# Both modulations at once, and the constants ahead of them, at the head of a two-layer adaLN kernel

## The chip, the cores and the metric

The kernel is one program for one core of a Trainium2 chip. The metric is the device time of one execution in microseconds (us). Three runs of the kernel before took 4933.53, 4936.85 and 4939.53 us; the median is 4936.85.

The engines are named as in the profile: PE is TensorE (PEld its weight loads), DVE is VectorE, ACT is ScalarE, POOL is GpSimd, and SP is the engine that issues all DMAs of this kernel.

## The reference

The state x has 4096 rows of 128 features, as two sequences of 2048 rows for the outer layers. Two layers, L0 and L1, each modulate a mixer ("attn") and a feed-forward model ("ffn") by a vector c:

```
mod = (silu(c) @ wmod).reshape(2, 6, 1, 128)         # c: 2 x 128, wmod: 128 x 768
sa, ca, ga, sb, cb, gb = mod[:, 0] ... mod[:, 5]
ga = (2*(ga >= 0) - 1) * max(|ga|, 0.25)              # gb the same
h = layernorm(x) * (1 + ca) + sa;   x = x + ga * attn(h)
h = layernorm(x) * (1 + cb) + sb;   x = x + gb * ffn(h)
```

The attention of L0 has 16 heads of 8 features and works on chunks of 64 rows: softmax attention inside a chunk, plus 0.1 times q times a memory matrix M per head. M is carried through the chunks by a delta rule, row by row: M = M - alpha * (M k) k^T + beta * v k^T, with k normalised to length 1, alpha = sigmoid(alpha_raw) * 0.5 and beta = sigmoid(beta_raw) * 2. The ffn of L0 is a model of six local attention layers with feed-forward parts; L1 has a linear attention and a model of two such layers.

## The kernel before

The program first makes a few constants (`ident`, `ones`, `onesm`, `nhalf`, `identb`, `cen`), then computes the modulation vectors of both layers, then the attention of L0 (`l0_attention`), then everything else in `local_models`. The change is in the first 90 us of the program.

**Modulation** (L130 to L159). `modulation(pre)` is called for L0 and then for L1, each with a memory pool of its own that is freed at its end. It loads `wmod` (128 x 768, 384 KB) and c (128 x 2), forms c * sigmoid(c) with an Exp on ACT (L136) and three small DVE operations (L137 to L140), does six matmuls (L143) into one PSUM bank, copies the 12 columns out (L147), adds 1 to two of the six vectors (L149), and applies the sign and floor rule to two others (L153 to L158, six DVE operations of 128 x 2 each). Since the second pool takes the memory of the first, the second load of `wmod` waits for the first modulation, and the attention's constants, whose pool takes the same memory, wait for the second.

**Constants of the attention** (L190 to L213). Six loads on SP: `wT` (the three projections' weights, 192 KB), `WoT`, `headsel`, `mask_chunk`, `na` (alpha, one value per partition), and `be` (beta, 128 values given to all 128 partitions). From `na` and `be` the two sigmoids are made (Exp on ACT at L200, then L201 to L203 on DVE), and from `wT` and `be` the weights `wkv` of the key and value projection (L212, L213).

**Projection stage** (L215 to L331). From `manual_schedule()` on (L216), each engine's order is the order in which the code is written; ahead of it, a scheduler orders the instructions. The 4096 rows are four groups of 1024 for the input norm and eight blocks of 512 for the rest:

- four loads of `xt` (128 x 8 x 128, 512 KB each, L318) on SP;
- `norm(g)`: the mean on DVE (`mu`, L238), the subtraction on POOL (`xn`, L241), a Square on ACT (`sq`, L243), the variance on DVE (`ve`, L245), the power -0.5 on POOL (`rt`, L248) and the product on POOL (`xn`, L249);
- `dims_first(blk)`: four transposes on PE of `xt` and four of `xn` (L257), ACT copies the first to `xb`, which SP stores to DRAM (`xD`, L127), and writes the modulated second to `hT` (L265);
- `project(blk)`: matmuls of `hT` with `wkv` (L274) and of `wT` with `hT` for q (L280), three ACT operations (`ksq` L284, `vt` L285, `qT` L286), a reduction and a polynomial for 1 / |k| on DVE (L289, L167 to L180) and the normalised key `kn` (L296);
- `keys(blk)`: four transposes of `kn` (L307), the ACT copy to `kT` (L308), and two DMAs on SP that regroup the keys through DRAM (`kdr` L309, `kr` L311).

The order of these steps is a written loop:

```
            norm(0)
            for j in range(-1, 9):
                if j in (-1, 1, 3):
                    norm((j + 3) // 2)
                if j + 1 < 8:
                    dims_first(j + 1)
                if 0 <= j < 8:
                    project(j)
                if 1 <= j:
                    keys(j - 1)
```

so that a norm's ACT operation stands in ACT's queue ahead of the copies of the block that follows it. `xt` and `xn` have four and two buffers; PSUM banks for the transposes, q and the keys are three, taken in turn.

**Behind the head.** The recursion over the rows of a chunk (`step`, L361 to L376, on DVE) begins when `kr` has been regrouped into `kd` (L347), beside the softmax attention of 32 tiles of 128 rows; then follow the chain over the chunks, the output projection, and the local models. Their order is written out by hand, too.

Of the kernel before, what the change touches and what calls it, by code (L numbers as in the profile page):

```python
# [72 lines left out]
def tile_kernel(ctx: ExitStack, tc: tile.TileContext, a: dict, out: bass.AP):  # L73
# [12 lines left out]
    @contextmanager  # L86
    def banks(name):

        with tc.tile_pool(name=name, bufs=2, space=PSUM) as p:
            cur[0] = p  # L90
            yield p
# [35 lines left out]
        nc.sync.dma_start(xD[:, blk * 512:(blk + 1) * 512], t)  # L127


    def modulation(pre):  # L130
        m = keep.tile([128, 6, 2], F32, name=f"{pre}_m")
        with tc.tile_pool(name=f"{pre}_modp", bufs=1) as mp, banks(f"{pre}_psm"):
            w = load(f"{pre}_wmod", (128, 768), mp)
            c = load(f"{pre}_cT", (128, 2), mp)
            e = mp.tile([128, 2], F32, name="e")
            nc.scalar.activation(e, c, AF.Exp, scale=-1.0)  # L136
            nc.vector.tensor_scalar(e, e, 1.0, None, ALU.add)  # L137
            s = mp.tile([128, 2], F32, name="s")
            nc.vector.reciprocal(s, e)
            nc.vector.tensor_tensor(s, s, c, ALU.mult)  # L140
            pm = ps("A")
            for k in range(6):
                nc.tensor.matmul(  # L143
                    pm[:, 2 * k:2 * k + 2], lhsT=w[:, k * 128:(k + 1) * 128], rhs=s,
                    start=True, stop=True,
                )
            nc.vector.tensor_copy(m.rearrange("p k b -> p (k b)"), pm[:, 0:12])  # L147
            for k in (1, 4):
                nc.vector.tensor_scalar(m[:, k, :], m[:, k, :], 1.0, None, ALU.add)  # L149
            for k in (2, 5):  # L150
                g = mp.tile([128, 2], F32, name="g")
                n = mp.tile([128, 2], F32, name="n")
                nc.vector.tensor_scalar(g, m[:, k, :], 0.0, 2.0, ALU.is_ge, ALU.mult)  # L153
                nc.vector.tensor_scalar(g, g, -1.0, None, ALU.add)
                nc.vector.tensor_scalar(n, m[:, k, :], -1.0, None, ALU.mult)
                nc.vector.tensor_tensor(n, n, m[:, k, :], ALU.max)
                nc.vector.tensor_scalar(n, n, 0.25, None, ALU.max)
                nc.vector.tensor_tensor(m[:, k, :], g, n, ALU.mult)  # L158
        return m  # L159


    def rsqrt_quick(scr, n, pool):
# [22 lines left out]

    def l0_attention(m):

        cp = ctx2.enter_context(tc.tile_pool(name="a_c", bufs=1))  # L190
        wT = load("L0_attn_wT", (128, 3, 128), cp)
# [20 lines left out]
        nc.vector.tensor_copy(wkv[:, 0], wT[:, 1, :])  # L212
        nc.vector.tensor_tensor(wkv[:, 1], wT[:, 2, :], be, ALU.mult)  # L213

        hp = ctx2.enter_context(tc.tile_pool(name="a_h", bufs=1))  # L215
        ctx2.enter_context(tc.manual_schedule())  # L216
        hT = hp.tile([128, T], F32, name="hT")
# [11 lines left out]
        with tc.tile_pool(name="a_p", bufs=2) as wp, tc.tile_pool(  # L229
            name="a_psP", bufs=2, space=PSUM  # L230
        ) as pp:
            P = {}

            def norm(g):

                xt = P["xt", g]
                mu = wp.tile([128, 8], F32, name="mu")
                nc.vector.tensor_reduce(mu, xt, AX.X, ALU.add)  # L238
                nc.vector.tensor_scalar(mu, mu, 1.0 / 128.0, None, ALU.mult)
                xn = P["xn", g] = wp.tile([128, 8, D], F32, name="xn")  # L240
                nc.gpsimd.tensor_tensor(xn, xt, bc(mu.unsqueeze(2), (128, 8, D)), ALU.subtract)  # L241
                sq = wp.tile([128, 8, D], F32, name="sq", bufs=1)
                nc.scalar.activation(sq, xn, AF.Square)  # L243
                ve = wp.tile([128, 8], F32, name="ve")
                nc.vector.tensor_reduce(ve, sq, AX.X, ALU.add)  # L245
                nc.vector.tensor_scalar(ve, ve, 1.0 / 128.0, 1e-5, ALU.mult, ALU.add)
                rt = wp.tile([128, 8], F32, name="rt")
                nc.gpsimd.tensor_tensor(rt, ve, bc(nhalf, (128, 8)), ALU.pow)  # L248
                nc.gpsimd.tensor_tensor(xn, xn, bc(rt.unsqueeze(2), (128, 8, D)), ALU.mult)  # L249

            def dims_first(blk):
                b = blk // NBLK
                ts_ = []
                for nm in ("xt", "xn"):
                    pt = pp.tile([128, 512], F32, tag="T", name="ps_x", bufs=3)
                    for c in range(4):
                        nc.tensor.transpose(  # L257
                            pt[:, c * 128:(c + 1) * 128],
                            P[nm, blk // 2][:, 4 * (blk % 2) + c, :], ident,
                        )  # L260
                    ts_.append(pt)
                xb = wp.tile([128, 512], F32, name="xb")
                nc.scalar.copy(xb, ts_[0])
                store_x(blk, xb)
                nc.scalar.activation(  # L265
                    hT[:, blk * 512:(blk + 1) * 512], ts_[1], AF.Identity,
                    bias=m[:, 0, b:b + 1], scale=m[:, 1, b:b + 1],
                )

            def project(blk):  # L270
                n0 = blk * 512
                pk = pp.tile([128, 4, 2, 128], F32, tag="K", name="ps_k")
                for c in range(4):
                    nc.tensor.matmul(  # L274
                        pk[:, c].rearrange("p s f -> p (s f)"),
                        lhsT=hT[:, n0 + c * 128:n0 + (c + 1) * 128],
                        rhs=wkv.rearrange("p s f -> p (s f)"), start=True, stop=True,
                    )
                pq = pp.tile([128, 512], F32, tag="T", name="ps_q", bufs=3)
                nc.tensor.matmul(  # L280
                    pq, lhsT=wT[:, 0, :], rhs=hT[:, n0:n0 + 512], start=True, stop=True
                )
                ksq = wp.tile([128, 4, 128], F32, name="ksq")
                nc.scalar.activation(ksq, pk[:, :, 0, :], AF.Square)  # L284
                nc.scalar.copy(vt[:, 4 * blk:4 * blk + 4, :], pk[:, :, 1, :])  # L285
                nc.scalar.mul(qT[:, n0:n0 + 512], pq, 1.0 / math.sqrt(8.0))  # L286

                ss = pp.tile([128, 4, 64], F32, tag="R", name="ps_r", bufs=1)
                nc.vector.tensor_reduce(  # L289
                    ss[:, 0], ksq.rearrange("p c (h d) -> p (c h) d", d=8), AX.X, ALU.add  # L290
                )
                rk = rsqrt_quick([ss[:, k] for k in range(4)], 64, wp)
                kn = P["kn", blk] = wp.tile([128, 4, 128], F32, name="kn")
                for c in range(4):
                    v = lambda t: t.rearrange("p (h d) -> p h d", d=8)
                    nc.vector.scalar_tensor_tensor(  # L296
                        v(kn[:, c]), v(pk[:, c, 0]), RSQ_C,
                        bc(rk[:, 16 * c:16 * c + 16].unsqueeze(2), (128, 16, 8)),
                        ALU.mult, ALU.mult,
                    )  # L300

            def keys(blk):
                sl = slice(blk * 512, (blk + 1) * 512)
                pt = pp.tile([128, 512], F32, tag="T", name="ps_kt", bufs=3)
                kn = P.pop(("kn", blk))
                for c in range(4):
                    nc.tensor.transpose(pt[:, c * 128:(c + 1) * 128], kn[:, c], ident)  # L307
                nc.scalar.copy(kT[:, sl], pt)  # L308
                nc.sync.dma_start(kdr[:, sl], kT[:, sl])  # L309
                v = kdr[0:16, sl]  # L310
                nc.sync.dma_start(  # L311
                    kr[blk:blk + 121:8, :, :],
                    bass.AP(v.tensor, v.offset, [[8 * T, 16], [T, 8], [1, 512]]),
                )

            for g in range(4):
                xt = P["xt", g] = wp.tile([128, 8, D], F32, name="xt", bufs=4)
                nc.sync.dma_start(  # L318
                    xt, a["x"][g * 1024:(g + 1) * 1024, :].rearrange("(c p) d -> p c d", p=128)
                )  # L320
            norm(0)
            for j in range(-1, 9):
                if j in (-1, 1, 3):
                    norm((j + 3) // 2)
                if j + 1 < 8:
                    dims_first(j + 1)
                if 0 <= j < 8:
# [3 lines that stand above are left out]
# [369 lines left out]
        assert done == len(todo)  # L700
        for f in finish(3):
            f()
        return E["hs"]

# [831 lines left out]
        while lsteps:  # L1538
            lstep()

    m0 = modulation("L0")
    m1 = modulation("L1")
    with ExitStack() as ctx2:
        hs0 = l0_attention(m0)
    with ExitStack() as ctx2:
        local_models(m0, m1, hs0)

# [62 lines left out]
```

## Time and profile before

| | us |
|---|---|
| median of three runs | 4936.85 |
| lowest and highest | 4933.53, 4939.53 |
| the profiled execution | 4928.13 |
| its span in the profile | 4926.3 |
| PE busy | 4493.8 (91%) |
| DVE busy | 3949.1 (80%) |
| POOL busy | 2781.2 (56%) |
| ACT busy | 2637.9 (54%) |
| first projection matmul starts | 34.99 |
| last `kT` copy starts | 87.06 |

The profile is of one execution. Times in its timeline count from the start of the span. Engines run their instructions in order; where an engine was idle before an instruction, the timeline gives the idle time and what released it, in brackets. The rows of windows give the length, then busy time with the number of instructions for PE, PEld, DVE, ACT and POOL, then the clock granted to PE, the share of the DMA engines that was busy, and GB/s. In this profile a matmul of two f32 operands is two records, a transpose one.

### The profile page before, as it was taken

What the parts mean: (1) busy time and instruction counts of PE and PEld (TensorE: products, weight loads), DVE (VectorE), ACT (ScalarE), POOL (GpSimd) and SP (SyncE); (2) the same over time, 40 slices, a digit from 0 to 9 for tenths busy, and PEclk for the clock granted to TensorE, in tenths of its full rate; (3) what the DMA queues carried; (4) which work ended last, traced back from release to release, by engine and by line L of the source; (5) the groups of instructions that cost most, each with busy time, mean ns of one, the idle gap of its engine ahead of it and who ended that gap; (6) DMA issues with size and microseconds to landing.
All of it is one profiled execution on the core that took longest, in us unless ns stands there. A gap on an engine that the chain in (4) does not pass through costs nothing.

```text
span 4926.3 us, 166334 instructions
## 1 busy us (share of the span) xinstructions
PE 4493.8 (91%) x73028; PEld 3066.5 (62%) x73058; DVE 3949.1 (80%) x6840; ACT 2637.9 (54%) x4207; POOL 2781.2 (56%) x1666
## 2 busy tenths in 40 slices
PE   5667799999999999999999999999999998899997
PEld 4445566666666666666666666666666665556554
DVE  6994488888888888888887888888877777788886
ACT  3223355555555555555555555555555555465554
POOL 3332366666666666666666666666655544455552
PEclk8778899999999999999999999999999999999999
DMA  2000222222222322223222322222212111111121
GB/s 78 1 1 25 85 65 67 69 73 70 69 65 64 87 68 65 66 73 76 68 64 64 79 72 65 66 74 69 68 51 59 50 51 46 37 46 49 51 58 41
DMA packets 222468, 295.31 MB, mean 60 GB/s; under 512 B 75657, under 2 KB 95409, under 8 KB 221745
## 3 DMA queue, kind: packets, MB, share of 16 engines
q1 hardware_dynamic: 221744, 284.67, 22.4%
q8 instruction: 576, 9.44, 0.8%
q14 instruction: 148, 1.20, 0.1%
HBM read 40.98 MB, written 10.75 MB: 10 GB/s over the span
## 4 chain that ended last, share of the span: by engine, by line
PE 49%; DVE 25%; ACT 7%; POOL 5%; issue 3%; DMA 0%; SPq 0%; POOLq 0%; DVEq 0%; ACTq 0%
PE ps_qk L871 12%; PE ps_o L1050 5%; PE ps_v L957 5%; DVE ps_qk L899 5%; PE ps_f L1150 5%; DVE t L888 5%; PE ps_turn L938 4%; PE ps_y L1067 4%; POOL r L894 4%; PE ps_s L997 3%; DVE r L883 3%; PE ps_fy L1175 3%; ACT sq L873 2%; DVE rs L1021 2%; PE ps_pT L1032 2%
## 5 line engine op out<-in xcount | busy, mean ns | idle before, releaser
L894 POOL TENSOR_TENSOR r<-r,t 128x1024 f32<-128x1024 f32 x448 | 1060.2, 2367 | 911.8 <-DVE t L888 794.3
L906 POOL TENSOR_TENSOR r<-r,rq_y 128x1024 f32<-128x1024 f32 x448 | 843.8, 1902 | 517.9 <-DVE rq_y L180 495.8
L873 ACT ACTIVATE sq<-ps_qk 128x1024 f32<-128x1024 f32 x448 | 460.6, 1028 | 1082.3 <-PE ps_qk L871 1014.7
L871 PE MATMUL ps_qk<-wp,hs 128*128 128x512 f32 x1792 | 893.8, 621 | 105.7 <-DVE rq_y L180 77.1
L883 DVE TENSOR_TENSOR r<-ps_qk,tb 128x1024 f32<-128x1024 f32 (+1 forms) x512 | 550.7, 1076 | 211.8 <-ACT sq L873 198.4
L1050 PEld LDWEIGHTS ps_o<-pT,v 64*64 64x64 f32 (+1 forms) x26624 | 479.4, 136 | 304.5 <-ACT pT L1033 160.9
L888 DVE TENSOR_TENSOR t<-ps_qk,tb 128x1024 f32<-128x1024 f32 (+1 forms) x512 | 554.1, 1082 | 143.1 <-POOL r L894 142.4
L1023 POOL TENSOR_TENSOR sm<-sm,rs 128x1024 f32<-128x1024 f32 x256 | 487.5, 1904 | 210.2 <-DVE rs L1022 126.9
L1050 PE MATMUL ps_o<-pT,v 64*64 64x32 f32 (+1 forms) x26624 | 531.2, 221 | 37.0 <-ACT pT L1033 19.2
L899 DVE TENSOR_REDUCE ps_qk<-sq 128x16 f32<-128x1024 f32 x448 | 549.0, 1226 | 11.9
L871 PEld LDWEIGHTS ps_qk<-wp,hs 128*128 128x128 f32 x1792 | 310.1, 193 | 364.3 <-issue 236.1
L938 PEld LDWEIGHTS ps_turn<-ident,r 128*128 128x128 f32 x3584 | 411.7, 143 | 125.2 <-issue 99.4
L957 PE MATMUL ps_v<-wp,hs 128*128 128x512 f32 x896 | 481.9, 639 | 1.0 <-ACT oT L1056 0.8
L1067 PEld LDWEIGHTS ps_y<-oT,wo 128*128 128x128 f32 x3584 | 430.2, 193 | 46.9 <-issue 42.5
L938 PE MATMUL ps_turn<-ident,r 128*128 128x128 f32 x3584 | 447.3, 277 | 9.7 <-POOL r L906 4.1
L1067 PE MATMUL ps_y<-oT,wo 128*128 128x128 f32 x3584 | 446.3, 276 | 1.5 <-ACT oT L1056 1.5
L1056 ACT COPY oT<-ps_o 128x512 f32<-128x512 f32 x448 | 244.0, 588 | 281.9 <-PE ps_o L1050 281.2
L1005 DVE TENSOR_REDUCE mx<-ps_s 128x16 f32<-128x1024 f32 (+1 forms) x256 | 312.5, 1221 | 97.4 <-PE ps_s L997 95.6
L997 PE MATMUL ps_s<-kT,qT 64*32 64x64 f32 (+1 forms) x26624 | 377.9, 230 | 0.7 <-issue 0.5
L997 PEld LDWEIGHTS ps_s<-kT,qT 64*32 64x32 f32 (+1 forms) x26624 | 325.8, 107 | 63.7 <-issue 53.0
L1150 PE MATMUL ps_f<-fx,w 128*128 128x512 f32 (+1 forms) x768 | 356.1, 600 | 2.5 <-DVE fx L1133 1.7
L1021 DVE TENSOR_REDUCE rs<-sm 128x16 f32<-128x1024 f32 (+1 forms) x256 | 310.5, 1213 | 51.1 <-ACT sm L1014 49.0
(265 smaller groups left out, 6850.5 us busy)
## 6 DMA issues: line engine op xcount, KB each, us to landing
v<-vn SPq DMA_DIRECT2D x1276, 128.0 KB
v<-vn SPq DMA_DIRECT2D x744, 64.0 KB
v<-vn SPq DMA_DIRECT2D x64, 256.0 KB
wp<-in_L_ffn_Wqkv SPq DMA_DIRECT2D x20, 512.0 KB
xD<-xb SPq DMA_DIRECT2D x24, 256.0 KB
xb<-xD SPq DMA_DIRECT2D x24, 256.0 KB
cs<-in_cos SPq DMA_DIRECT2D x128, 32.0 KB
cs<-in_sin SPq DMA_DIRECT2D x128, 32.0 KB
```

The source lines that it names most:

```text
L871: nc.tensor.matmul(pq[:, js], lhsT=hw, rhs=wts[g, u][:, js], start=True, stop=True)
L883: nc.vector.tensor_tensor(r[:, es].rearrange("p (h d) -> p h d", d=DH), pq[:, es].rearrange("p (h d) -> p h d", d=DH), bc(tb[:, 0, s].unsq ...
L888: nc.vector.tensor_tensor(t2[:, es].rearrange("p (h s d) -> p h s d", s=2, d=32), pq[:, es].rearrange("p (h s d) -> p h s d", s=2, d=32)[: ...
L894: nc.gpsimd.tensor_tensor(r, r, t2, ALU.add)
L899: nc.vector.tensor_reduce(pq[:, 16 * v:16 * v + 16], st[i].pop(("sq", v)).rearrange("p (h d) -> p h d", d=DH), AX.X, ALU.add,)
L906: nc.gpsimd.tensor_tensor(rv, rv, bc(y[:, 16 * v:16 * v + 16].unsqueeze(2), (128, 16, DH)), ALU.mult)
L938: nc.tensor.transpose(p[:, c * 128:(c + 1) * 128], r[:, cs], ident)
L957: nc.tensor.matmul(p, lhsT=hw, rhs=wv, start=True, stop=True)
L997: nc.tensor.matmul(sp[W * w:W * w + W, c0:c0 + 2 * W], lhsT=qT[64 * q:64 * q + 64, cc, W * w:W * w + W], rhs=kT[64 * q:64 * q + 64, cc, W ...
L1050: nc.tensor.matmul(po[s][64 * q:64 * q + 64, 128 * c + W * w:128 * c + W * w + W], lhsT=v2[kp, w, co:co + 64], rhs=pT[kp, q, c, W * w:W * ...
L1067: nc.tensor.matmul(py[:, 0:128], lhsT=wts[g, "o"][:, c * NO + s, :], rhs=oT[:, s, c, :], start=(c + s == 0), stop=(c == 3 and s == NO - 1),)
L1150: nc.tensor.matmul(ps_[c][0:sz], lhsT=wts[g, "w1"][:, o:o + sz], rhs=S["x"], start=True, stop=True,)
```

## The change

One function now makes both modulations. It loads c and `wmod` of both layers, does each small operation once on 128 x 4 values instead of twice on 128 x 2, does the twelve matmuls one after another, and leaves both results in one tile. It is called inside `l0_attention`, behind the loads and the preparation of the attention's constants and ahead of the projection stage. The second and third input norm are given out one turn of the loop sooner, and `xn` has four buffers instead of two.

```diff
-    def modulation(pre):
-        m = keep.tile([128, 6, 2], F32, name=f"{pre}_m")
-        with tc.tile_pool(name=f"{pre}_modp", bufs=1) as mp, banks(f"{pre}_psm"):
-            w = load(f"{pre}_wmod", (128, 768), mp)
-            c = load(f"{pre}_cT", (128, 2), mp)
-            e = mp.tile([128, 2], F32, name="e")
+    def modulation():
+        m = keep.tile([128, 2, 6, 2], F32, name="m")
+        with tc.tile_pool(name="modp", bufs=1) as mp, banks("psm"):
+            c = mp.tile([128, 2, 2], F32, name="c")
+            ws = []
+            for i, pre in enumerate(("L0", "L1")):
+                nc.sync.dma_start(c[:, i, :], a[f"{pre}_cT"])
+                ws.append(load(f"{pre}_wmod", (128, 768), mp))
+            e = mp.tile([128, 2, 2], F32, name="e")
             nc.scalar.activation(e, c, AF.Exp, scale=-1.0)
...
             pm = ps("A")
-            for k in range(6):
-                nc.tensor.matmul(
-                    pm[:, 2 * k:2 * k + 2], lhsT=w[:, k * 128:(k + 1) * 128], rhs=s,
-                    start=True, stop=True,
-                )
-            nc.vector.tensor_copy(m.rearrange("p k b -> p (k b)"), pm[:, 0:12])
+            for i in range(2):
+                for k in range(6):
+                    o = 12 * i + 2 * k
+                    nc.tensor.matmul(
+                        pm[:, o:o + 2], lhsT=ws[i][:, k * 128:(k + 1) * 128], rhs=s[:, i, :],
+                        start=True, stop=True,
+                    )
+            nc.vector.tensor_copy(m.rearrange("p i k b -> p (i k b)"), pm[:, 0:24])
             for k in (1, 4):
-                nc.vector.tensor_scalar(m[:, k, :], m[:, k, :], 1.0, None, ALU.add)
+                nc.vector.tensor_scalar(m[:, :, k, :], m[:, :, k, :], 1.0, None, ALU.add)
             for k in (2, 5):
...
-        return m
+        return m[:, 0], m[:, 1]
...
-    def l0_attention(m):
+    def l0_attention():
...
         nc.vector.tensor_tensor(wkv[:, 1], wT[:, 2, :], be, ALU.mult)
 
+        m, m1 = modulation()
         hp = ctx2.enter_context(tc.tile_pool(name="a_h", bufs=1))
...
-                xn = P["xn", g] = wp.tile([128, 8, D], F32, name="xn")
+                xn = P["xn", g] = wp.tile([128, 8, D], F32, name="xn", bufs=4)
...
-                if j in (-1, 1, 3):
-                    norm((j + 3) // 2)
+                if j in (-1, 0, 2):
+                    norm({-1: 1, 0: 2, 2: 3}[j])
...
-        return E["hs"]
+        return E["hs"], m, m1
...
-    m0 = modulation("L0")
-    m1 = modulation("L1")
     with ExitStack() as ctx2:
-        hs0 = l0_attention(m0)
+        hs0, m0, m1 = l0_attention()
```

More of the change, by code (lines that the diff above doesn't have):

```diff
@@ L127, in store_x @@
         nc.sync.dma_start(xD[:, blk * 512:(blk + 1) * 512], t)
-    def modulation(pre):
-        m = keep.tile([128, 6, 2], F32, name=f"{pre}_m")
-        with tc.tile_pool(name=f"{pre}_modp", bufs=1) as mp, banks(f"{pre}_psm"):
-            w = load(f"{pre}_wmod", (128, 768), mp)
-            c = load(f"{pre}_cT", (128, 2), mp)
-            e = mp.tile([128, 2], F32, name="e")
+    def modulation():
[7 more added lines that the diff above has]
+            e = mp.tile([128, 2, 2], F32, name="e")
             nc.scalar.activation(e, c, AF.Exp, scale=-1.0)
             nc.vector.tensor_scalar(e, e, 1.0, None, ALU.add)
-            s = mp.tile([128, 2], F32, name="s")
+            s = mp.tile([128, 2, 2], F32, name="s")
             nc.vector.reciprocal(s, e)
@@ L141, in modulation @@
             pm = ps("A")
-            for k in range(6):
-                nc.tensor.matmul(
-                    pm[:, 2 * k:2 * k + 2], lhsT=w[:, k * 128:(k + 1) * 128], rhs=s,
-                    start=True, stop=True,
-                )
-            nc.vector.tensor_copy(m.rearrange("p k b -> p (k b)"), pm[:, 0:12])
+            for i in range(2):
[6 more added lines that the diff above has]
+            nc.vector.tensor_copy(m.rearrange("p i k b -> p (i k b)"), pm[:, 0:24])
             for k in (1, 4):
-                nc.vector.tensor_scalar(m[:, k, :], m[:, k, :], 1.0, None, ALU.add)
+                nc.vector.tensor_scalar(m[:, :, k, :], m[:, :, k, :], 1.0, None, ALU.add)
             for k in (2, 5):
-                g = mp.tile([128, 2], F32, name="g")
-                n = mp.tile([128, 2], F32, name="n")
-                nc.vector.tensor_scalar(g, m[:, k, :], 0.0, 2.0, ALU.is_ge, ALU.mult)
+                v = m[:, :, k, :]
+                g = mp.tile([128, 2, 2], F32, name="g")
+                n = mp.tile([128, 2, 2], F32, name="n")
+                nc.vector.tensor_scalar(g, v, 0.0, 2.0, ALU.is_ge, ALU.mult)
                 nc.vector.tensor_scalar(g, g, -1.0, None, ALU.add)
-                nc.vector.tensor_scalar(n, m[:, k, :], -1.0, None, ALU.mult)
-                nc.vector.tensor_tensor(n, n, m[:, k, :], ALU.max)
+                nc.vector.tensor_scalar(n, v, -1.0, None, ALU.mult)
+                nc.vector.tensor_tensor(n, n, v, ALU.max)
                 nc.vector.tensor_scalar(n, n, 0.25, None, ALU.max)
-                nc.vector.tensor_tensor(m[:, k, :], g, n, ALU.mult)
-        return m
+                nc.vector.tensor_tensor(v, g, n, ALU.mult)
+        return m[:, 0], m[:, 1]
     def rsqrt_quick(scr, n, pool):
```

## The prediction

> **What bounds the kernel now.** I read the page first, then the stage windows, then the timeline of the first 90 us. The page's chain of work that ended last is TensorE and VectorE almost alone, and spread over the FFN stages:
>
> ```profile
> PE 49%; DVE 25%; ACT 7%; POOL 5%; issue 3%; DMA 0%; SPq 0%; POOLq 0%; DVEq 0%; ACTq 0%
> ```
>
> The change touches the first 87 us, 1.8% of the span. The windows (busy us per engine, instructions in brackets) show what is idle there:
>
> ```profile
> 0.00:35.00 35.00, 9.01 (x41) 8.58 (x41) 16.21 (x60) 7.04 (x11) 11.52 (x12) 0.93 0.40 108
> 35.00:90.00 55.00, 39.51 (x161) 28.69 (x162) 35.08 (x130) 25.77 (x46) 13.62 (x9) 0.81 0.28 93
> 90.00:200.00 110.00, 69.91 (x853) 44.66 (x862) 100.23 (x130) 37.03 (x77) 44.34 (x24) 0.73 0.02 7
> ```
>
> In the first 35 us no engine is busy half of the time: it is a chain of waits. From 90 us on VectorE is busy 100 of 110 us in a fixed order. So a head that ends earlier shifts what follows, and nothing there takes it back. The timeline shows the head's chain (start, duration, line, idle before and releaser):
>
> ```profile
> 6.66 1.22 DVE L238 TENSOR_REDUCE mu<-xt 128x8 f32<-128x1024 f32 x1 [2.05 <-DMA xt<-in_x]
> 8.22 2.72 PE L143 MATMUL ps_A<-s,c_L_wmod 128*128 128x2 f32 x12 [8.22 <-DVE s L140]
> 13.38 0.34 SPq L98 DMA_DIRECT2D c_L_wmod<-in_L_wmod  x1
> 20.36 2.69 PE L143 MATMUL ps_A<-s,c_L_wmod 128*128 128x2 f32 x12 [9.42 <-issue]
> 26.23 0.33 SPq L98 DMA_DIRECT2D c_L_attn_wT<-in_L_attn_wT  x1
> 28.50 0.43 SPq L197 DMA_DIRECT2D be<-in_L_attn_b  x1
> 32.75 0.31 ACT L200 ACTIVATE be<-be 128x128 f32<-128x128 f32 x1 [2.27 <-DMA be<-in_L_attn_b]
> 34.99 3.75 PE L274 MATMUL ps_k<-wkv,hT 128*128 128x256 f32 x8 [8.04 <-issue]
> 38.78 0.60 ACT L284 ACTIVATE ksq<-ps_k 128x512 f32<-128x512 f32 x1 [5.72 <-PE ps_k L274]
> 46.76 1.06 ACT L243 ACTIVATE sq<-xn 128x1024 f32<-128x1024 f32 x1 [5.68 <-POOL xn L241]
> 62.63 1.06 ACT L243 ACTIVATE sq<-xn 128x1024 f32<-128x1024 f32 x1 [5.93 <-POOL xn L241]
> 87.06 0.58 ACT L308 COPY kT<-ps_kt 128x512 f32<-128x512 f32 x1 [3.86 <-PE ps_kt L307]
> ```
>
> Reading: the second modulation's weights start only at 13.38, when the first has freed its memory, and the attention's constants at 26.23, when the second has. The last constant, `be`, lands 4.25 us after its issue, and only then is `wkv` made and the first projection started (34.99). After that two stalls stand out: the Squares of norms 2 and 3 sit in ScalarE's queue ahead of the copies of a block that is ready, and ScalarE waits 5.68 and 5.93 us for GpSimd's subtraction. The head ends with the last `kT` copy at 87.06; the next GpSimd, VectorE and TensorE work of the recursion follows within 0.7 us.
>
> **The change, part by part.** The instruction streams of the two built programs tell more than the diff. Behind the head all five streams are the same, instruction for instruction. In the head SP now issues six constants, then c, weights, c, weights, and the four `xt` tiles last. VectorE does all constants, then both modulations, and the first `mu` only after eleven of the fifteen small operations that follow the modulation matmuls. ScalarE has Square 1 ahead of block 0's copies and Square 2 ahead of block 1's; Square 3 comes one block sooner.
>
> Step 1, constants. The first issue is at 0.73 as now; `be` is sixth, 2.27 us later (26.23 to 28.50), at 3.0, and lands at 7.25 by its own 4.25 us. Lower bound: the load before it took 2.25 (issued 28.03, used 30.28). Upper bound: its row plus 1.3 us for a 384 KB weight tile mixed into it at the 290 GB/s seen around 9 us, 8.6. I take its own row, since it is the same transfer. The second c is issued at 4.4 and lands 3.0 later (1.19 to 4.20 now, also behind weights), at 7.4. [...]
>
> Step 2, VectorE's chain behind `be`: 32.75 to 34.89 is 2.14 us; into it go the sigmoid's add, the casts of `ident` and `cen` (0.44 together) and the reciprocal and product (0.42). TensorE starts the modulations at 10.25.
>
> Step 3, matmuls. Now 12 records take 2.72 and 2.69 us, beside other work. Together they are 24 in a row, with VectorE's copy, the gates and `mu` queued behind: 5.4 us if all run at the pace of now. From 34.99 on TensorE ran at half clock (granted 0.50) and was back at full pace 5.2 us later; in the stall after 64.21 it took 3.5. If it comes after 3.5 us here, the 24 take 4.45. I take 4.9: copy at 15.2. [...]
>
> Step 4, from the copy to `mu`: 10.98 to 12.48 now, less 0.34 for two casts that are elsewhere now, plus one operation: 1.24. `mu` starts at 16.45 instead of 6.66. Its `xt` has long landed: 1.13 MB stand ahead of it and 0.5 MB are its own, 6 us at the 260 to 290 GB/s of the windows from 2 us on, with a us or two for landing.
>
> Step 5, norms. `mu` to the subtraction is 1.51 now, with two small operations between 1.67: 18.1. GpSimd's round of a norm is 1.92 to the Square, 1.09, 1.51, 1.71 (norm 2's rows: 44.84, 46.76, 47.85, 49.36, 51.07) and 1.85 to the next subtraction, 8.08. Norms 0 and 1 pass, so norm 2 subtracts at 34.3 and its Square runs at 36.2. Block 0's Square of keys follows 2.10 later as now (46.76 to 48.86): 38.3, against 38.78. So the earlier constants by themselves bring half a microsecond: what they free is spent on the later `mu` and on norm 2, which is now in front.
>
> Step 6, stalls. Norm 2's stall behind block 0 is gone. Block 1's matmuls start when block 1's `hT` is out (36.2 plus 2.21) and one transpose set is through (1.1): 39.5; they take 3.75 at half clock, 1.89 at full; as TensorE has worked since 38, I take 3.1. Its Square runs at 42.65, `kn` ends 4.6 later, `mu` 3 starts at 47.15, Square 3 at plus 3.48 (59.15 to 62.63): 50.65. That stall stays. From it to the end were 24.43; one more block now lies behind it, 4.08 by the steps of `kT` (70.87, 74.98, 79.04): end at 79.15.
>
> Sum: 87.06 less 79.15, a gain of 7.9 us. The profiled execution took 4928.13 (span 4926.3), so it would be 4920.2; the median of the runs shown is 4936.85, 8.7 above it, and the gain, being a shift of everything behind, is taken from that: 4929.0.
>
> Edits at nothing: the four buffers of `xn` remove a wait on TensorE that was over anyway; the later `xt` issues wait for earlier loads' lanes, `xt` 3 for `be` at 7.25, needed at 47, and behind it in SP's queue only stores wait that are due after 20; SP's stores lag 0.8 us behind the last `kT` and with one more unstalled block perhaps 1.2, while the gather of `kr`, issued at 92.24, is not read before 102.29. If that cover were gone, a later `kr` would delay VectorE one for one.
>
> With all short ends (step 1 less 1.0, matmuls less 0.45, block 1's matmuls less 0.4) the gain is 9.75; with all long ones (1.3, 0.5, 0.65) 5.4.
>
> **Rivals.** Short head: the short ends hold together, and the extra block takes 3.57 (`kT` 79.04 to 82.61) instead of 4.08: gain 10.3, 4926.6. For it: `be` is the only constant that took over 2.5 us, and a store went beside it. Against: four things have to go one way.
>
> One load after another: SP's ten loads ahead of `xt`, instead of overlapping, each wait for the one before; five at 2.3, `be` 4.25, two c at 2.3, two weights near 3.0 and `xt` 5.0 (1.65 to 6.66) put `mu` near 32. The head is then 15.6 longer than forecast and the kernel 7.7 slower, 4944.5. It turns to a loss from a `mu` at 24.3. Against: now six such loads were issued in 2.27 us and all landed within 4.3 us of the last issue.
>
> Every tile behind the head lies 32 bytes lower in the built program, because one tile of 96 bytes replaces two of 48 padded to 64. If operands in other places were slower by 1% on VectorE's quarter of the chain (1230 us), 12.3 us are lost and the kernel is 4.4 slower, 4941.3; if faster, it is 20 us faster, 4916.7. It decides from 0.64%. Against: `fsq` lies on both kinds of places, and its 96 writes (L1100) took 574 to 644 ns, median 589.
>
> Change without effect: if norm 2's stall were only moved, 87.06 would shift by the half microsecond of step 5: 4936.3.
>
> **Numbers.** A measurement of this kernel can tell about 0.2%, 9.9 us, from no change; my gain is below that. Forecast 0.55, short head 0.29, other places 0.03 each way, one after another 0.04, no effect 0.06. Faster is the short head, the places that help, and 0.01 of the forecast read high (runs spread by 6 us): 0.33. Of the 0.07 of the two losing cases, whose sizes have no upper bound, I put 0.05 beyond 9.9 us: slower 0.05. The rest, with 0.02 of these, is same: 0.62. The sum's ends give 4927.1 to 4931.5; with 3 us of spread and the reach to the other cases the range is 4923 to 4935.
>
> **What would show it.** Step 1: `be` used near 7.3. Steps 2 to 4: 24 records from about 10.3, `mu` near 16.5. Step 5: Square 2 near 36, after a long wait of ScalarE. Step 6: one stall near 51 instead of two. Last `kT` near 79, and every stage behind it as long as now. Wrong would be a `mu` before 14 or after 19, a second stall, or stages behind the head of another length.

## The result: 0.18% less, from a head that is 8.6 us shorter

| | before | after |
|---|---|---|
| median of 11 runs each, same chip | 4935.9 | 4925.99 |
| lowest and highest | 4927.92, 4940.96 | 4919.22, 4936.02 |
| profiled execution | 4928.13 | 4920.01 |
| its span | 4926.3 | 4918.2 |
| last `kT` copy starts | 87.06 | 78.45 |

The ratio of after to before is 0.9982, 95% interval 0.9973 to 0.999: some 9 us, with 5 and 13 as ends. That is within the 0.2% that was named as what can be told from no change, as forecast; the median is 3.0 us below the predicted 4929.0 and inside the range.

### The profile after

The chain that ended last is still TensorE and VectorE, and still lies in the FFN stages:

```profile
PE 47%; DVE 26%; ACT 7%; POOL 5%; issue 4%; DMA 1%; SPq 0%; POOLq 0%; DVEq 0%; ACTq 0%
```

The same three windows as before (length; busy us and instructions of PE, PEld, DVE, ACT, POOL; granted clock; DMA share; GB/s):

```profile
0.00:35.00 35.00, 12.99 (x50) 10.84 (x50) 13.93 (x44) 5.26 (x8) 12.67 (x13) 1.00 0.36 101
35.00:90.00 55.00, 38.45 (x169) 25.54 (x170) 37.70 (x132) 27.87 (x49) 15.43 (x10) 0.78 0.33 111
90.00:200.00 110.00, 68.61 (x920) 46.96 (x926) 104.64 (x137) 37.40 (x78) 45.13 (x24) 0.78 0.00 1
```

The first 35 us are as empty as before: no engine is busy for more than 40% of them. The third window is fuller for VectorE (104.64 against 100.23), because the recursion, which packs it, begins sooner. The timeline shows the head's chain, step by step as the prediction has it:

```profile
6.68 0.31 ACT L207 ACTIVATE be<-be 128x128 f32<-128x128 f32 x1 [1.76 <-DMA be<-in_L_attn_b]
7.98 0.20 ACT L139 ACTIVATE e<-c 128x4 f32<-128x4 f32 x1 [1.00 <-DMA c<-in_L_cT]
9.39 5.28 PE L148 MATMUL ps_A<-s,c_L_wmod 128*128 128x2 f32 x24 [9.39 <-DVE s L143]
14.71 0.18 DVE L152 COPY m<-ps_A 128x24 f32<-128x24 f32 x1 [5.37 <-PE ps_A L148]
16.09 1.21 DVE L246 TENSOR_REDUCE mu<-xt 128x8 f32<-128x1024 f32 x1
17.61 1.90 POOL L249 TENSOR_TENSOR xn<-xt,mu 128x1024 f32<-128x1024 f32 x1 [16.31 <-DVE mu L247]
35.73 1.06 ACT L251 ACTIVATE sq<-xn 128x1024 f32<-128x1024 f32 x1 [5.89 <-POOL xn L249]
37.84 0.60 ACT L292 ACTIVATE ksq<-ps_k 128x512 f32<-128x512 f32 x1
38.55 3.20 PE L282 MATMUL ps_k<-wkv,hT 128*128 128x256 f32 x8
41.80 0.60 ACT L292 ACTIVATE ksq<-ps_k 128x512 f32<-128x512 f32 x1 [1.24 <-PE ps_k L282]
49.73 1.06 ACT L251 ACTIVATE sq<-xn 128x1024 f32<-128x1024 f32 x1 [5.62 <-POOL xn L249]
78.45 0.58 ACT L316 COPY kT<-ps_kt 128x512 f32<-128x512 f32 x1 [3.48 <-PE ps_kt L315]
```

What to see: the first projection's Square of keys (37.84) has no idle time in front of it; it is held by the Square at 35.73 that stands ahead of it in ScalarE's queue, not by its matmuls. One stall of 5.62 us is left ahead of the last `kT`, at 49.73, where before had two behind the first block.

Behind the head nothing gives the gain back at once. The last `z` step comes 297.4 us after the last `kT` copy (297.0 before), so it starts at 375.9 instead of 384.1. The span is 8.1 us shorter.

### The profile page after: what moved, and what is told of

The parts are those of the page before. It is cut to its first block, busy times and chain, and to the rows that moved or that the text cites. A ratio compares the mean times of both kernels' runs of the same rounds, so it can differ in the third digit from the quotient of the medians.

```text
span 4918.2 us, 166304 instructions
## 1 busy us (share of the span) xinstructions
PE 4474.6 (91%) x73028; PEld 3055.6 (62%) x73058; DVE 3946.2 (80%) x6822; ACT 2635.7 (54%) x4206; POOL 2780.6 (57%) x1666
## 4 chain that ended last, share of the span: by engine, by line
PE 47%; DVE 26%; ACT 7%; POOL 5%; issue 4%; DMA 1%; SPq 0%; POOLq 0%; DVEq 0%; ACTq 0%
PE ps_qk L879 11%; PE ps_o L1058 5%; DVE ps_qk L907 5%; DVE t L896 5%; PE ps_f L1158 5%; PE ps_v L965 5%; PE ps_turn L946 4%; POOL r L902 4%; PE ps_y L1075 4%; DVE r L891 3%; PE ps_s L1005 3%; PE ps_fy L1183 3%; ACT sq L881 2%; DVE rs L1029 2%; PE ps_pT L1040 2%
## 5 line engine op out<-in xcount | busy, mean ns | idle before, releaser
L907 DVE TENSOR_REDUCE ps_qk<-sq 128x16 f32<-128x1024 f32 x448 | 549.0, 1225 | 11.9
```

What stands on the lines that cost most here:

```text
L907: nc.vector.tensor_reduce(pq[:, 16 * v:16 * v + 16], st[i].pop(("sq", v)).rearrange("p (h d) -> p h d", d=DH), AX.X, ALU.add,)
```

## The experiments

In all of them nothing of the computation is left out. The start of the last `kT` copy is followed, the end of the head; it can be read from one profile: the two kernels that differ from before and from after in the place of tiles alone ended the head at 86.67 and 79.00, within 0.6 us of 87.06 and 78.45. The time can't, as the table at the end of this section shows.

### The norms alone

```
 before.py, with
-                xn = P["xn", g] = wp.tile([128, 8, D], F32, name="xn")
+                xn = P["xn", g] = wp.tile([128, 8, D], F32, name="xn", bufs=4)
-                if j in (-1, 1, 3):
-                    norm((j + 3) // 2)
+                if j in (-1, 0, 2):
+                    norm({-1: 1, 0: 2, 2: 3}[j])
```

> The kernel before with the norms given out a block sooner and four xn buffers; constants behind the modulations as before. Followed is the start of the last copy into kT, which ends the head: 87.06 us in before, 78.45 in after. Theory: the two parts of the change shorten one and the same chain of ScalarE work, so the norm order alone brings most of it. The constants and K0 stay where before has them (first Square of keys at 38.8), the 5.9 us for which ScalarE waited for the third input group's subtraction goes, and the last copy into kT starts at about 79.4. Rival: the constants, there some 8 us sooner, are what starts the head sooner; then without them the last copy stays near 87.

Measured: 83.42, between the two; a gain of 3.64 us, not 7.7. ScalarE's timeline:

```profile
30.93 1.06 ACT L243 ACTIVATE sq<-xn 128x1024 f32<-128x1024 f32 x1 [4.86 <-POOL xn L241]
33.12 0.30 ACT L200 ACTIVATE be<-be 128x128 f32<-128x128 f32 x1
41.75 0.60 ACT L284 ACTIVATE ksq<-ps_k 128x512 f32<-128x512 f32 x1 [8.33 <-PE ps_k L274]
53.56 1.06 ACT L243 ACTIVATE sq<-xn 128x1024 f32<-128x1024 f32 x1 [6.05 <-POOL xn L241]
83.42 0.58 ACT L308 COPY kT<-ps_kt 128x512 f32<-128x512 f32 x1 [3.39 <-PE ps_kt L307]
```

The stall behind the first block is gone, but the first Square of keys comes at 41.75 instead of 38.78. Nothing waited for `be` to land; its sigmoid now stands behind the third group's Square on ScalarE, and on VectorE the rest of it behind that group's variance. The stall has turned into an 8.33 us wait for `ps_k`: from the first Square of keys to the end 6.61 us are gained (48.28 us before, 41.67 here), and 2.97 are lost ahead of it.

### The head alone

```
 after.py, with
-                xn = P["xn", g] = wp.tile([128, 8, D], F32, name="xn", bufs=4)
+                xn = P["xn", g] = wp.tile([128, 8, D], F32, name="xn")
-                if j in (-1, 0, 2):
-                    norm({-1: 1, 0: 2, 2: 3}[j])
+                if j in (-1, 1, 3):
+                    norm((j + 3) // 2)
```

> The kernel after with the norms back at blocks 1 and 3 and two xn buffers; both modulations at once and the constants ahead of them stay. Theory: with the old order the chain has slack only until the third group's norm; hT0 at 29, first Square of keys at 33.1, the Square of the third group at about 41, last copy into kT at about 81.4, which is 5.7 us below before: with the norms alone at 7.7 and both at 8.6, the parts do not add. Rival, the prediction's step for the constants as a term of its own that adds to the norms' gain: the constants alone bring about 0.5 to 0.9 us, last copy at 86.2 to 86.6.

Measured: 82.03, a gain of 5.03 us; the theory's number was near, the rival's far off.

```profile
33.61 0.60 ACT L292 ACTIVATE ksq<-ps_k 128x512 f32<-128x512 f32 x1 [2.63 <-PE ps_k L282]
41.60 1.06 ACT L251 ACTIVATE sq<-xn 128x1024 f32<-128x1024 f32 x1 [6.38 <-POOL xn L249]
82.03 0.58 ACT L316 COPY kT<-ps_kt 128x512 f32<-128x512 f32 x1 [3.43 <-PE ps_kt L315]
```

Everything from the first Square of keys on (33.61, before 38.78) is 5 us sooner, and the stall behind the first block stays (6.38). With the last run this makes a square: the constants bring 5.03 us with the old order and 4.97 with the new (83.42 to 78.45); the norms bring 3.64 and 3.58. The parts add, which my theory had denied. With the sooner constants, too, the sooner norm delays the first Square of keys (33.61 to 37.84), and gains more behind it.

The times of these two runs stand the other way round: 4926.09 for the norms alone, 4941.72 for the head alone, though its head is 1.4 us shorter. Windows of TensorE alone, from the last `z` step on (length, busy and instructions, granted clock, DMA share, GB/s), first of the norms alone, then of the head alone:

```profile
380.80:450.00 69.20, 51.42 (x664) 0.77 0.10 28
```

```profile
379.40:450.00 70.60, 55.42 (x630) 0.67 0.10 27
```

In a stage with the same instructions the second got a lower clock (0.67) and did 630 of them where the first did 664; the stage to the first Square of the FFN took 202.0 us instead of 192.2.

### The places of the tiles

```
 before.py, with
+    mm = keep.tile([128, 2, 6, 2], F32, name="m")
-        m = keep.tile([128, 6, 2], F32, name=f"{pre}_m")
+        m = mm[:, int(pre[1])]
```

> The kernel before with the two modulations' results in one tile of 96 bytes a partition, as after has them, so that every later tile in SBUF lies 32 bytes lower, as in after; the instructions and their order are those of before. Theory: places cost nothing; last copy into kT at 87.06, the stages behind it as long as in before, ratio to before within 0.1% of 1. [...]

```
 after.py, with
-        m = keep.tile([128, 2, 6, 2], F32, name="m")
+        m32 = keep.tile([128, 32], F32, name="m")
+        m = m32[:, 0:24].rearrange("p (i k b) -> p i k b", i=2, k=6)
```

> The kernel after with its 96 bytes of modulation results in a tile of 128 bytes a partition, so that every later tile in SBUF lies where before has it; instructions and order as in after. Theory: places cost nothing, and the time follows the head: last copy into kT at 78.45, ratio to before 0.9973 to 0.999, the interval that after gave. Rival: the 32 bytes have a price in the long stages; by the borderline ratio of the places run, 1.0011, after would be held back by some 5 us, and with the old places the ratio would come out near 0.997, 14 us below before.

Measured: before with the lower places, ratio 1.0011 (1.0 to 1.0022); after with the old places, 0.9982 (0.997 to 0.9995), the same number as after's own. A price of 12 us, which the prediction's rival named, is excluded by both. The first alone would have left a doubt of 5 us. The second shows no sign of it, but doesn't exclude it: after with the old places would then be near 0.9972, just inside its interval.

### The fourth group's norm in two pieces

```
 after.py, with norm(g) cut into norm_a (mean, subtraction) and norm_b (the rest)
+                if j == 1:
+                    norm_a(3)
+                if j == 2:
+                    norm_b(3)
```

> The kernel after with the fourth group's norm given out in two pieces: mean and subtraction at block 1, the Square and what follows at block 2. Theory: the 5.6 us for which ScalarE stands idle before the fourth group's Square (49.7 in after) is the time of the subtraction behind it on GpSimd, on the path of the head; with the subtraction given out a block sooner the Square starts at about 46, the last copy into kT at 73 to 75, and the span is 3.5 to 5.5 us shorter than after's. Rival: another wait takes its place (the transposes' PSUM banks, or GpSimd's own work for the third group, which the sooner subtraction delays), and the last copy stays within 1 us of 78.45.

```profile
45.70 1.06 ACT L254 ACTIVATE sq<-xn 128x1024 f32<-128x1024 f32 x1 [0.79 <-POOL xn L249]
73.20 0.59 ACT L319 COPY kT<-ps_kt 128x512 f32<-128x512 f32 x1 [3.48 <-PE ps_kt L318]
```

The stall is 0.79 us instead of 5.62 and the head 5.25 us shorter. What ScalarE waited for was the subtraction's place in the order, and no other wait took over.

### The first input group first

```
 after.py, with the loads and the order of the head written out by hand
+            load_xt(0)                       # ahead of every other load
+            # in short: loads of wT, be, c, wmod, c, wmod, then the small ones and xt 1 to 3
+            norm_a(0)                        # ahead of the constants' VectorE work
+            # in short: the modulations' matmuls; norm_sq(0); norm_b(0); norm_a(1); copy of m
```

> The kernel after with the order of the head written out by hand on every queue: the first input group is loaded first of all, and its mean and subtraction run ahead of the modulations (first subtraction at about 6 us instead of 17.6); the constants still come ahead of the modulations; the norms come at the same blocks as in after. Theory: what starts the head in after is not the modulations' result but the place of the first norm behind them, 11.4 us for which ScalarE has nothing to do before the first Square (19.5 in after); with the norm first, the first Square comes at about 8, the first Square of keys at 27 to 29 instead of 37.84, and the last copy into kT at 67 to 69.5, the span 9 to 11.5 us below after's. Rival: the modulations' own chain (loads, exp, 24 weight loads, copy) still decides when hT0 can be written; hT0 then comes no sooner than now less the 3 us that the later modulations allow, and the last copy stays at 76 to 78.

And with the norms in pieces as well:

```
+                if j == -1:
+                    norm_a(2)
+                if j == 1:
+                    norm_sq(2); norm_b(2); norm_a(3)
+                if j == 3:
+                    norm_sq(3); norm_b(3)
```

> As the last one, and with the norms given out in pieces: the third group's mean and subtraction at block -1, its Square, multiplication and the fourth group's mean and subtraction at block 1, the fourth group's Square and the rest at block 3, so that ScalarE never waits for a subtraction. Theory: all ScalarE waits of 5 us and more behind the first Square of keys go; the last copy into kT comes at 58 to 61, the span is 17 to 21 us below after's and about 26 to 29 below before's, ratio to before 0.9938 to 0.995. Rival: from some point the matmuls or VectorE set the pace of a block (4.1 us a block in after's even stretch), so that the waits taken away come back as waits for K and the transposes; last copy at 65 or later, ratio to before 0.9955 or more.

> The kernel with the first input group first and the norms in pieces, without the transposes, timed again beside it, for a closer ratio than its six runs gave (0.9938, 0.992 to 0.9956). Theory: a shift of everything behind a head that is 27.4 us shorter; ratio 0.9935 to 0.9953. Rival: part of the first ratio was chance, ratio above 0.9955.

Measured: 69.59 for the first, 0.1 us past its bounds, with its first Square of keys at 28.81 as said, and 59.65 and 59.83 for the second. Of the second, with the fourth group's Square:

```profile
8.22 1.04 ACT L228 ACTIVATE sq<-xn 128x1024 f32<-128x1024 f32 x1
35.53 1.06 ACT L228 ACTIVATE sq<-xn 128x1024 f32<-128x1024 f32 x1
59.65 0.59 ACT L350 COPY kT<-ps_kt 128x512 f32<-128x512 f32 x1 [3.29 <-PE ps_kt L349]
```

The first Square runs at 8.22 (19.5 in after), and the fourth has no wait in front of it. Both theories hold: it is the place of the first norm behind the modulations, and then the stalls, that make the head of after long. The ratio to before is 0.9938 (0.992 to 0.9956) in six runs and 0.9949 (0.9933 to 0.9964) in six others; medians 4900.5 and 4907.27 beside 4930.89 and 4933.33. This is the version that beats both kernels: 27.2 to 27.4 us off the head, and that much, within the intervals, off the time.

### Throwaway work ahead of the modulation matmuls

```
 after.py with 32; the version with the first input group first, in pieces, with 76; in modulation()
+            pw = ps("A")
+            for k in range(32):
+                nc.tensor.transpose(pw[:, 0:128], ident, ident)
             pm = ps("A")
```

> The kernel after with 32 throwaway transposes of the identity on TensorE ahead of the modulations' matmuls, into a PSUM bank of their own; they run while TensorE waits for the loads. Theory, on the step of the prediction that was read 0.4 us short: the 24 modulation records took 5.28 us in after because TensorE had only begun to work; if it has been at work for several us before, they run at full pace and take 2.6 to 2.9, the copy of m comes at about 12.2 instead of 14.71, the first mu, subtraction and Square 2.5 sooner, and the last copy into kT at 75.5 to 76.2. Rival: 128 x 128 weight loads for two moving columns set the pace of these records whatever the clock is; they take 5.3 us again, and the last copy stays at 78.4, or comes later where the transposes hold the matmuls up.

> The kernel with the first input group first and the norms in pieces, and 76 throwaway transposes of the identity on TensorE ahead of the modulations' matmuls, enough to keep it at work until just before them; the order on every other queue is written out by hand and stays the same, which it did not in the first run with such transposes. Theory: the 24 modulation records take 2.7 to 3.1 us instead of 5.28 (weight loads near 186 ns instead of 333), their copy comes 2 us or more sooner than 15.52, and the head does not follow, because the first hT waits for the second Square and that for GpSimd (17.27): last copy into kT at 59.1 to 59.9. Rival: the modulations' result is on the path there too, and the last copy comes 1.5 to 2.5 us sooner than 59.65, at 57.2 to 58.2.

The summaries of the modulations' weight loads (minimum, median and maximum in ns, first and last start), in after, with 32 transposes, and with 76:

```profile
L148 PEld LDWEIGHTS ps_A<-s,c_L_wmod x24: 285/333/334, 9.4 to 14.2; 128*128 128x128 f32 x24
```

```profile
L151 PEld LDWEIGHTS ps_A<-s,c_L_wmod x24: 186/330/333, 10.0 to 13.8; 128*128 128x128 f32 x24
```

```profile
L152 PEld LDWEIGHTS ps_A<-s,c_L_wmod x24: 190/192/192, 12.1 to 14.7; 128*128 128x128 f32 x24
```

With 76 transposes, which ended at 12.2, all 24 loads run at 190 to 192 ns and the records take 2.74 us: the 333 ns of after are not what such a load needs by itself. With 32, TensorE stood idle from 6.55 to 10.05, the loads began at 186 ns and fell to 333, and the records took 4.20. The prediction of that run was half wrong, and its head (74.55) can't be put down to the records: VectorE's order, which the scheduler makes there, had changed, too, with the first `mu` at 11.97, as soon as `xt` landed. In the run with 76, where the order is written, the last copy came at 59.15, as the theory said. But the copy of m came only 0.55 us sooner (14.97, was 15.52) and not 2, because the matmuls waited for the transposes, and the head came half a microsecond sooner with it; by the end of the head alone the rival isn't settled. The rows settle it:

```profile
15.19 1.46 DVE L159 TENSOR_SCALAR m<-m 128x4 f32<-128x4 f32 x2
16.59 1.06 ACT L231 ACTIVATE sq<-xn 128x1024 f32<-128x1024 f32 x1 [6.96 <-POOL xn L227]
18.02 0.78 ACT L310 ACTIVATE hT<-ps_x,m 128x512 f32<-128x512 f32 x1
```

What the first `hT` (18.02) needs of m was ready at 16.65; `hT` stands behind the second Square, which waited for GpSimd until 16.59 (17.27 without the transposes). So the modulations are off the path once the input comes first, with 1.4 us to spare, and the half microsecond comes with GpSimd's second subtraction (14.66, was 15.34).

> The kernel of the last run again, timed: its head ended at 59.1 us, as early as any, but its single execution took 4931.1 us, 30 longer than the same kernel without the transposes (4900.5 median). Theory: the single execution fell among the long ones of a spread of 20 us and more that the stages behind the head have in every kernel; ratio to before 0.992 to 0.996. Rival: the transposes' work on TensorE at the start makes the clock that is granted later lower, and the time is lost behind the head: ratio 0.997 to 1.0.

> The kernel with the first input group first and the norms in pieces, with 76 throwaway matmul records on TensorE as in the run with 76 transposes, but small ones (64 x 32 weights, 32 columns), so that the number of instructions and their place in the program are the same and the array's work is a small part. It asks what of the throwaway transposes lengthened the stages behind the head: ratio to before 0.9978 (0.9966 to 0.999) with them, 0.9949 (0.9933 to 0.9964) without, at a head that is 0.6 us shorter with them. Theory: their work did, through the clock that is granted later; with the small ones the ratio is 0.993 to 0.996. Rival: 76 more instructions on TensorE's queue did, by where they put the program behind them; the ratio is 0.997 to 0.999 again. Third: the difference was chance, and the ratio says nothing of either.

The single time of the run with 76 transposes, 4931.09, was a long one of its kernel (eleven runs: 4911.98 to 4932.7, median 4921.38), but the kernel is slower, too: timed, its ratio is 0.9978 (0.9966 to 0.999), some 14 us worse than the same kernel without, at a head of 59.13. With 76 small records in their place (38 matmuls of `ident[0:64, 0:32]`, two records each) it is 0.9993 (0.998 to 1.0006), at a head of 59.23. So the loss doesn't follow the array's work, which was 11.0 us with the transposes and 4.3 with the small records: the 76 records more bring it, as the rival had it, with even more than it gave. Why they do, by the place of the program behind them or otherwise, is not shown. Waits of TensorE from 600 us to 4950 at the local attention's output matmuls, 26624 of them, for nothing that the profile shows (us in total, times, longest), in before, after, the best version, and with 76 transposes and 76 small records:

```profile
PE ps_o L1050 <- issue: 16.7, 25, 1.5
```

```profile
PE ps_o L1058 <- issue: 15.7, 20, 1.7
```

```profile
PE ps_o L1096 <- issue: 11.9, 18, 1.6
```

```profile
PE ps_o L1099 <- issue: 21.3, 29, 2.2
```

```profile
PE ps_o L1099 <- issue: 23.4, 31, 1.8
```

The three profiles with 76 extra records have 21 to 23 us of such waits, the eleven others 10 to 18. These waits are some 10 us of the loss beside the best version (11.9 and 12.7 in its two profiles), but only 5 to 7 beside before. The rest of it, and whether it is the program's place in memory, stays open: no run moved the program without adding instructions.

### What one execution can tell

Lengths in each profile, in us: the head; from the last `z` step to the first Square of the FFN; from there to the first matmul of L1's attention on its state; the span.

| kernel | head | to the Square | to L1 | span |
|---|---|---|---|---|
| before | 87.06 | 186.1 | 3008.3 | 4926.3 |
| after | 78.45 | 187.3 | 3005.8 | 4918.2 |
| norms alone | 83.42 | 192.2 | 3006.5 | 4924.3 |
| head alone | 82.03 | 202.0 | 3011.2 | 4939.9 |
| before, lower places | 86.67 | 201.6 | 3004.0 | 4938.1 |
| after, old places | 79.00 | 193.0 | 3010.9 | 4928.8 |
| fourth norm in pieces | 73.20 | 192.2 | 3004.1 | 4912.0 |
| input first | 69.59 | 193.6 | 2998.6 | 4902.8 |
| input first, in pieces | 59.65 | 194.9 | 3000.6 | 4894.9 |
| the same again | 59.83 | 198.9 | 3010.5 | 4917.6 |
| with 32 transposes | 74.55 | 193.7 | 3004.4 | 4913.9 |
| with 76 transposes | 59.15 | 201.3 | 3018.1 | 4929.3 |
| the same again | 59.13 | 190.5 | 3017.0 | 4916.8 |
| with 76 small records | 59.23 | 194.8 | 3026.0 | 4932.7 |

The second column differs by 16 us over the same instructions, the third by 13 without the last three rows, the kernels with 76 extra records, whose third column is the longest of all. One pair of executions can't show 8 us; the head's end can.

## Why the prediction was right

**Steps 1 and 2** were close and a little long: `be` was issued at 3.06 (3.0) and used at 6.68 (7.25); its landing took 3.6 us and not the 4.25 of its own row in before, and in four other kernels with this order of loads it was used at 6.22 to 6.75. The second c, issued at 4.49 and used at 7.98 (7.4), came later than forecast and decided as much as `be`: its Exp ended at 8.18, just as VectorE came free of the reciprocal of `be` (8.23). In the other kernels VectorE then stood idle for c, 0.2 to 0.6 us. No run shows the 1.0 us that the range's short end takes off step 1: in the five kernels `be` was used at 6.22 at the earliest, and in after the matmuls started 0.86 us sooner than forecast. From `be` to the matmuls it was 2.71 us and not 3.0; they started at 9.39 (10.25).

**Step 3** was short: 5.28 us against 4.9. No record sped up: the weight loads took 333 ns in the median and 285 at the least. The copy came at 14.71 (15.2).

**Steps 4 and 5** held: from the copy to `mu` 1.38 us (1.24), from `mu` to the subtraction 1.52 (1.67), to the third group's Square 18.12 (18.1), to the first Square of keys 2.11 (2.10); 37.84 against 38.3.

**Step 6** held in kind: one stall instead of two, `mu` 3 at 46.31 (47.15), the Square at 49.73 (50.65), and from there 28.72 us to the end (28.5). Of what was put at nothing, SP's stores lagged more, 2.2 us behind the last `kT` copy and not 1.2, and the cover held: `kr` was issued at 84.97 and read at 93.68. The sum is 8.61 us against 7.9. The mis-sized terms are the start of the modulations' matmuls, forecast 0.86 too late, their length up to the copy, 0.37 too short, the way from the third group's Square to block 1's projection, 0.48 too long (2.82 us, because the transposes ahead of it ran at full pace in 0.63 and not in 1.1), and the last stretch, 0.22 too short: 0.75 us together, of which the small terms between them take 0.05 back.

**One sentence of step 5 is wrong:** "So the earlier constants by themselves bring half a microsecond: what they free is spent on the later `mu` and on norm 2." By themselves they bring 5.03 us. The half microsecond compares the first Square of keys in the two kernels, and in after that instruction waits for the third group's Square, not for the constants. A step's own gain was read from a place on the chain where the other part of the change had already taken over. The sum was not hurt, because it followed the whole chain.

**The rivals.** One load after another: ten loads were issued between 0.73 and 5.4, and `mu` had no DMA to wait for. Other places: no price found, and 12 us excluded. No effect: refuted, at 8.6 us of head. Short head: of its four short ends one came, the start of the matmuls (0.86 of 1.0); the records, block 1's matmuls (3.20 us, not 2.7) and the extra block did not, and the gain of the head lies between it and the forecast.

**The time.** The gain was taken from a median of three runs, 4936.85. The forecast's own execution was met within 0.2 us (4920.2 against 4920.01), in part by luck, since the spans of one kernel differ by 20 us; the median came 3.0 below forecast.

## What to carry to other kernels

Cost the parts of a change one at a time from the order each alone would make, and then together: here the sum was right and the share of a part wrong by a factor of ten. In a written order, look at where a wait's producer stands, too: giving out a subtraction a block sooner than its Square took 5.25 us off after's head, and the first norm ahead of the modulations, in another run, 8.9. Over the same instructions behind the change, the stretch to the first Square of the FFN differed by 16 us here, so follow the edited stage in the trace, and time both kernels many times on one chip.

## What was not expected of the hardware

Some small VectorE operations took as long as a GpSimd operation on 128 x 1024 beside them still ran. In after one operation took 0.16 us at 15.74, with GpSimd idle, and 1.84 at 17.68, beside a subtraction that began at 17.61 and ended at 19.51:

```profile
17.68 1.84 DVE L164 TENSOR_TENSOR m<-g,n 128x4 f32<-128x4 f32 x1
```

In the run with the norms alone one of them lay on the path, the product that ends beta's sigmoid, 1.94 us instead of 0.22. The same form beside GpSimd's power `rt`, of 128 x 8, and a reciprocal in the same trace took 0.22 and 0.17 us:

```profile
33.66 1.82 POOL L248 TENSOR_TENSOR rt<-ve,nhalf 128x8 f32<-128x8 f32 x1 [2.77 <-DVE sel L205]
34.35 0.22 DVE L201 TENSOR_SCALAR be<-be 128x128 f32<-128x128 f32 x1
35.56 1.90 POOL L249 TENSOR_TENSOR xn<-xn,rt 128x1024 f32<-128x1024 f32 x1
35.59 1.94 DVE L203 TENSOR_SCALAR be<-be 128x128 f32<-128x128 f32 x1
18.19 1.90 POOL L241 TENSOR_TENSOR xn<-xt,mu 128x1024 f32<-128x1024 f32 x1
18.29 0.17 DVE L139 RECIPROCAL s<-e 128x2 f32<-128x2 f32 x1
```

So a GpSimd operation beside it does not always lengthen a VectorE operation: of these rows two lasted until GpSimd's ended (1.84 and 1.94 us), and two did not (0.22 and 0.17). What sets them apart is shown by no run here.

The granted clock in the profile's rows does not show the slow start. In the window from 9 to 15 us of after it stands at 1.00 while the weight loads take 333 ns; the run with 32 transposes shows it fall, with the pace of the records (the count in brackets):

```profile
10.50:11.00 0.50, 0.50 (x7) 1.00 1.18 334
11.00:11.50 0.50, 0.50 (x5) 0.77 1.20 305
11.50:12.00 0.50, 0.50 (x4) 0.50 1.18 287
```

In windows of 0.5 us, 32 transposes sped up about 3.2 us after they began (from 4 or 5 a window to 7) and 76 about 5.2 us after (the same counts), and the records behind the 32 slowed about 4.6 us after the transposes had ended (from 7 a window to 4). After's 24 records did not speed up in their 5.28 us. No single delay fits these numbers, and no run here shows what sets it.
